# The second attention of a four-block network: where the softmax division is done, and who fixes the order of the vector engines

## The chip, the core and the metric

The kernel runs on one core of one Trainium2 chip. The core has five engines that take their instructions from queues of their own: TensorE (PE in the profile; PEld is its weight load), VectorE (DVE), ScalarE (ACT), GpSimd (POOL) and SyncE (SP, which issues transfers). The metric is the device time of one execution in microseconds; a comparison uses the median of several executions.

## The reference

Six residual blocks follow each other on 8 sequences of 512 rows with 256 columns, all in fp32. The change touches the fifth block, the second kind of attention, and what runs beside it. Each row is normalised first, and the block adds its result to the normalised rows:

```
def _L1_attn_ref(x, w_q, w_k, w_v, w_o):        # 16 heads of 64
    q = jnp.einsum('bsd,hdk->bhsk', x, w_q)
    k = jnp.einsum('bsd,hdk->bhsk', x, w_k)
    v = jnp.einsum('bsd,hdk->bhsk', x, w_v)
    scores = jnp.einsum('bhqk,bhmk->bhqm', q, k) * scale
    weights = jax.nn.softmax(scores, axis=-1)
    z = jnp.einsum('bhqm,bhmk->bhqk', weights, v)
    ...
    return x + z            # z after its heads are joined and multiplied by w_o
...
    x = x + 0.5 * _L1_ffn_ref(_layernorm(x), ...)       # the block before: 16 experts, 4 per row
    x = x + _L1_attn_ref(_layernorm(x), ...)
    x = x + 0.5 * _L1_ffn_ref(_layernorm(x), ...)       # the block after
```

There is no mask. The blocks before and after route every row to 4 of 16 experts; the rows are scattered to slots in memory, multiplied tile by tile, and gathered again.

## The kernel before

The rows stay on the chip in `x` as 32 tiles of 128 rows. `_attn1` (L925) works through 64 chunks; chunk n = 8b + c holds heads 2c and 2c+1 of sequence b. A chunk has two halves of two query tiles each, and the half numbered g = 2n + half is the unit of the loop (L1119 to L1155).

What one chunk needs:

- `heads` (L984): two projections `pq` (L992), the queries copied out by ACT (L998), the keys by DVE (L1000). They are made two chunks ahead.
- `scores` (L1005): per query tile the score matmuls of both heads (L1018) into a pair of banks `sp`, the negated row maxima on DVE (L1024), and two exponentials on ACT (L1027), which also sum each row.
- `turn` (L1032): the exponentials of a query tile are transposed on TensorE (L1039), four blocks per bank for each head, and copied into `eT`. `evict` (L186 to L189) gives head 0 to DVE and head 1 to ACT.
- `products` (L1042): `run` multiplies `eT` with the values (L1052) and lets GpSimd widen the reciprocals of the sums (L1059). `scale` transposes these on TensorE (L1065), copies them with ACT (L1069) and multiplies the product by them on DVE (L1071).
- `value` (L967) and `project` (L1076): the value projections of the coming sequence (L973, copied at L977), and the output projections of the previous one (L1082, added to `x` at L1086).
- `prepare` (L938): the means and variances of some tiles (`ln_range`), normalised rows (L952), `x` plus these rows on GpSimd (L958), and their transposes (L961).

Scores run a half ahead: `scores(g + 1)` is issued before the turns of half g. The products of chunk n are issued in the first half of chunk n + 1, between its scores and its first turn. Projections wait in a list `fill`; one is taken between the two turns of a half, and in each half a share of the rest after the second turn. Two pairs of banks hold scores, one bank the product `zp`, and all turns and projections rotate through three banks with the tag "m".

Other work runs beside it. During the first chunks, results of the block before are added to `x` on DVE (`add`, L1443), four per chunk, each followed by an indirect gather on GpSimd (L1424). In chunk 42 the means, and in chunks 43 to 47 the normalised rows, transposes and logits of the first 20 tiles of the next block are made (`Front.units`, L1817); from chunk 48 on the steps of its `routing` (L1260) run on DVE, five per chunk; in the last 20 halves GpSimd scatters rows (`send`, L1245).

The order on TensorE and GpSimd is the order in which the program issues (`manual_schedule`, L1113). DVE's and ACT's instructions are ordered by the compiler's planner; the adds of L1443 carry one order by hand, behind the last row maximum (`latest`, `behind`).

## Time and profile before

| | |
|---|---|
| median of 3 executions | 4506.57 us (4497.96 to 4514.63) |
| the profiled execution | 4405.38 us, its span 4403.7 us |
| granted clock of TensorE, mean over the span | 0.916 |
| the second attention, first transpose to last output projection | 2655.8 to 3952.8 us |
| PE, PEld, DVE, ACT, POOL busy over the whole span | 88%, 52%, 45%, 33%, 28% |

The profiled execution is about 100 us shorter than the median of the others; the profile doesn't show those. All rows of the profile are of this one execution. In the page, a group gives the line, the engine, the operation, the output and input tiles and their shapes, the count, the busy time with the mean duration in ns, and the idle time of the engine just before, with what ended it. A wait is named by the instruction that waited and the one that ended it. A line of the trace in order of time gives the start, the duration, engine, line and operation, and in brackets the idle time before it. Matmuls overlap, so their durations are latencies: the spacing of weight loads shows their rate.

### The profile page before, as it was taken

To read this page: it belongs to the slowest core of one execution; us is meant where nothing else is said; L and a number is where in the kernel's file an instruction comes from. 1 tells how busy PE (TensorE), PEld (TensorE's weight loads), DVE (VectorE), ACT (ScalarE), POOL (GpSimd) and SP (SyncE) were. 2 spreads that over 40 slices of the span, in tenths; PEclk is the share of its full clock that TensorE was granted. 3 is DMA by queue.
4 is the path that set the end of the run, shared out by engine and by line. 5 is a ranking of instruction groups with operands and counts; after the bars stand their busy time and mean duration, and the time that the engine had idled before them with its cause. 6 is when DMAs were issued, how large, how long until landed. Compare 5 with 4: busy or idle time off the path is not lost.

```text
span 4403.7 us, 51503 instructions
## 1 busy us (share of the span) xinstructions
PE 3892.5 (88%) x17660; PEld 2305.1 (52%) x17660; DVE 1966.9 (45%) x5201; ACT 1437.6 (33%) x3226; POOL 1225.5 (28%) x1132
## 2 busy tenths in 40 slices
PE   5799987999999769999678988999999999998988
PEld 5566653333334546656445664545545555556664
DVE  5221116545554441210464455665555547455355
ACT  2122222433433212222122233544454443442331
POOL 2323323323320223233253141220000020542156
PEclk9999997889996579999689999999999999998999
DMA  5223226500000313232433450100000000133464
GB/s 181 54 59 67 69 38 227 174 22 11 25 20 6 97 34 64 63 66 39 132 121 120 163 177 25 29 27 8 1 1 1 1 1 1 48 115 123 149 187 134
DMA packets 262992, 316.64 MB, mean 72 GB/s; under 512 B 31696, under 2 KB 232784, under 8 KB 262480
## 3 DMA queue, kind: packets, MB, share of 16 engines
q1 hardware_dynamic: 213584, 212.12, 15.4%
q0 software_dynamic: 49152, 101.24, 9.5%
q8 instruction: 145, 2.38, 0.2%
q14 instruction: 111, 0.91, 0.1%
HBM read 157.81 MB, written 147.06 MB: 69 GB/s over the span
## 4 chain that ended last, share of the span: by engine, by line
PE 35%; DVE 7%; issue 4%; DMA 3%; ACT 3%; POOL 1%; SPq 0%; POOLq 0%; DVEq 0%; ACTq 0%
PE pq L992 5%; PE hs L1651 5%; PE sp L1018 5%; PE zp L1052 5%; PE tp L1039 4%; PE pv L973 3%; PE yp L1082 2%; DMA yg<-ys_d,slot 2%; ACT ex L1027 2%; DVE nmax L1024 1%; PE hp L1571 1%; POOL yg L1424 1%; PE yps L1671 1%; DMA acc_d<-ob,idx 1%; DVE xT L189 1%
## 5 line engine op out<-in xcount | busy, mean ns | idle before, releaser
L1027 ACT ACTIVATE ex<-sp,nmax 128x512 f32<-128x512 f32 x512 | 347.3, 689 | 411.5 <-DVE nmax L1024 389.8
L458 PE MATMUL op<-w,hid 128*128 128x256 f32 x2048 | 473.3, 394 | 0.0
L447 PE MATMUL hp<-exT,w 128*128 128x512 f32 x1024 | 447.5, 595 | 0.0
L458 PEld LDWEIGHTS op<-w,hid 128*128 128x128 f32 x2048 | 406.2, 199 | 66.6 <-issue 8.6
L1424 POOL DMA_INDIRECT yg<-ys_d,slot x256 | 262.9, 1027 | 514.5 <-DVE x L1443 222.9
L465 POOL DMA_INDIRECT acc_d<-ob,idx x128 | 199.7, 1560 | 688.6 <-ACT ob L464 383.8
L1651 PE MATMUL hs<-w_sb,xT 128*128 (+1 forms) x1152 | 338.5, 418 | 54.6 <-DVE xT L189 46.0
L463 DVE TENSOR_TENSOR ob<-op,b 128x256 f32<-128x256 f32 x128 | 54.4, 425 | 663.3 <-PE op L458 656.6
L1024 DVE TENSOR_REDUCE nmax<-sp 128x2 f32<-128x1024 f32 x256 | 303.2, 1218 | 72.8 <-PE sp L1018 72.7
L1039 PEld LDWEIGHTS tp<-ident,ex 128*128 128x128 f32 x2048 | 227.6, 142 | 190.8 <-issue 129.6
L447 PEld LDWEIGHTS hp<-exT,w 128*128 128x128 f32 x1024 | 194.7, 192 | 232.0 <-issue 231.2
L1039 PE MATMUL tp<-ident,ex 128*128 128x128 f32 x2048 | 276.2, 278 | 36.3 <-ACT eT L187 35.9
L735 DVE CUSTOM_DVE_ANT_0 junk<-sp,mask 128x128 f32<-128x128 f32 (+3 forms) x512 | 248.7, 486 | 130.1 <-PE sp L728 110.5
L1651 PEld LDWEIGHTS hs<-w_sb,xT 128*128 128x128 f32 x1152 | 205.7, 198 | 175.7 <-DVE xT L189 96.4
L451 ACT ACTIVATE hid<-hp,b 128x512 f32<-128x512 f32 x256 | 175.9, 687 | 337.9 <-PE hp L447 337.9
L1018 PE MATMUL sp<-qk,qk 64*128 64x512 f32 x1024 | 261.4, 630 | 2.2 <-ACT ex L1027 2.2
L1245 POOL DMA_INDIRECT slots_d<-wide,slot x176 | 174.1, 989 | 309.7 <-DMA slots_d<-wide,slot 113.1
L992 PE MATMUL pq<-xnT,wide 128*128 128x512 f32 x512 | 251.2, 614 | 5.8 <-DVE eT L189 5.0
L773 ACT ACTIVATE ex<-st 128x1024 f32<-128x1024 f32 (+3 forms) x256 | 173.9, 703 | 245.6 <-DVE st L771 245.5
L1052 PE MATMUL zp<-eT,v 128*64 128x512 f32 x1024 | 234.9, 600 | 0.3 <-DVE eT L189 0.3
L464 ACT ACTIVATE ob<-ob,gate 128x256 f32<-128x256 f32 x128 | 65.0, 508 | 510.8 <-DVE ob L463 510.8
L1059 POOL COPY wide<-rec 128x512 f32<-128x512 f32 x64 | 39.3, 614 | 672.5 <-PE rp L1065 577.2
(328 smaller groups left out, 6105.9 us busy)
## 6 DMA issues: line engine op xcount, KB each, us to landing
xs<-slots_d SPq DMA_DIRECT2D x70, 512.0 KB, 5.1
ys_d<-ys SPq DMA_DIRECT2D x70, 512.0 KB, 3.5
w<-in_W SPq DMA_DIRECT2D x32, 1024.0 KB, 5.6
slots_d<-mask SPq DMA_DIRECT2D x8, 2304.0 KB, 14.7
ys_d<-mask SPq DMA_DIRECT2D x8, 2304.0 KB, 13.0
w_sb<-in_w SPq DMA_DIRECT2D x24, 512.0 KB, 7.8
xn_d<-xn SPq DMA_DIRECT2D x16, 512.0 KB, 4.3
acc_d<-x SPq DMA_DIRECT2D x8, 1024.0 KB, 5.7
```

Source lines behind the costliest of these rows:

```text
L447: nc.tensor.matmul(hp, lhsT=w1[:, c, f * P : f * P + P], rhs=exT[e][:, c, h * CH : h * CH + CH], start=(c == 0), stop=(c == DC - 1),)
L458: nc.tensor.matmul(op, lhsT=hid[h][:, f, i * P : i * P + P], rhs=w2[:, f, :], start=(f == 0), stop=(f == FC - 1),)
L465: nc.gpsimd.indirect_dma_start(out=acc_d[:, :], out_offset=bass.IndirectOffsetOnAxis(ap=idx[:, e, st : st + 1], axis=0), in_=ob, in_offset ...
L735: nc.vector.tensor_tensor_reduce(out=junk[:, :wd], in0=sps[h // 2][:, h % 2, :wd], in1=mask[:, S - wd :], scale=1.0, scalar=NEG, op0=ALU.a ...
L992: nc.tensor.matmul(pp, lhsT=(wq, wk)[a][:, k, c * P : c * P + P], rhs=seq[b]["xnT"][:, k, :], start=(k == 0), stop=(k == DC - 1),)
L1018: nc.tensor.matmul(sp[:, j, :], lhsT=q[r, qt * P : qt * P + P], rhs=k[r, :], start=True, stop=True)
L1024: latest[0] = nc.vector.tensor_reduce(nmax, sp, AX.X, ALU.max, negate=True).ins
L1027: nc.scalar.activation(ex[:, j, :], sp[:, j, :], AF.Exp, bias=nmax[:, j : j + 1], accum_out=ch["sums"][:, qt, j : j + 1],)
L1039: nc.tensor.transpose(tp[:, k, :], ch["ex", qt][:, j, k * P : k * P + P], self.ident)
L1052: nc.tensor.matmul(zp[DK1 * j : DK1 * j + DK1, :], lhsT=seq[b]["v", h][:, k, at : at + DK1], rhs=ch["eT"][:, j, k, :], start=(k == 0), sto ...
L1424: inst = nc.gpsimd.indirect_dma_start(out=self.y[t][:, r, :], out_offset=None, in_=self.k.ys_d[:, :], in_offset=bass.IndirectOffsetOnAxis( ...
L1651: nc.tensor.matmul(hp.rearrange("p a i -> p (a i)"), lhsT=st[j]["xT"][:, c, :], rhs=self.w13[:, st[j]["e"], c, :].rearrange("p e i -> p (e ...
```

## The change

The exponentials are divided by their row sums before they are turned. `divide(i)` takes the reciprocal of a query tile's two sums and multiplies both heads' rows in place on DVE. The reciprocals' widening, transposes, copy and the product on DVE go; the product `zp` is copied out by ACT (`out`). `evict` gives the turns of even query tiles to DVE and of odd ones to ACT.

The order of DVE and ACT is now that of the program too. In a half: scores and maxima of the next half with the exponentials of its first tile, the products or the adds, the even turn, the exponentials of its second tile, the copy of the product, one step beside, one projection, the first division, the odd turn, a step, the other projections, the second division, a step. The adds move from the first half to the second and start in chunk 0.

Means of `x` that were taken in one go (`ln_range` at sequences 3 and 5, and `Front.stats`) are taken two tiles at the end of a chunk (`own`). A sequence's normalisation, transposes, value projections and the output projections are spread over its chunks by a fixed table: normalisation at c = 0, transposes at c = 1, values 2, 1, 1, 2, 1, 1 at c = 2 to 7, output projections two at c = 1 and two at c = 2. Routing runs six steps per chunk.

```diff
@@ -938,24 +938,22 @@
         def prepare(b):
             st = seq[b] = {"z": []}
-            def norm(c):
+            def normal():
+                mv, rstd = stats
+                st["xn"] = work.tile([P, QT, D], F32, name="xn", bufs=1)
+                st["xnT"] = work.tile([P, DC, CH], F32, name="xnT")
 ...
+                rows = self.x[:, b * QT : b * QT + QT, :]
+                nc.gpsimd.tensor_tensor(rows, rows, st["xn"], ALU.add)
+            def turned(c):
                 def run():
-                    mv, rstd = stats
-                    if c == 0:
-                        if b in (0, 3, 5):
-                            self.ln_range(pool, stats, b * QT, {0: 3, 3: 2, 5: 3}[b] * QT)
-                        st["xn"] = work.tile([P, QT, D], F32, name="xn", bufs=1)
-                        st["xnT"] = work.tile([P, DC, CH], F32, name="xnT")
 ...
-                        nc.gpsimd.tensor_tensor(rows, rows, st["xn"], ALU.add)
                     tp = psum.tile([P, CH], F32, name="tpn", tag="m", bufs=3)
                     for i in range(QT):
                         nc.tensor.transpose(
@@ -977,9 +975,10 @@
                     nc.vector.tensor_copy(st["v", h][:, i, :], pp)
                 return run
-            return [norm(c) for c in range(DC)] + [
-                value(i, h) for h in range(HK // CH) for i in range(QT)
-            ]
+            v = [value(i, h) for h in range(HK // CH) for i in range(QT)]
+            return [[normal], [turned(0), turned(1)], v[0:2], v[2:3], v[3:4], v[4:6], v[6:7], v[7:8]]
         def heads(n):
             b, c = divmod(n, NC)
@@ -1004,11 +1003,10 @@
         def scores(g):
             n, half = divmod(g, 2)
             ch, q, k = chunk[n], chunk[n][0], chunk[n][1]
-            if half == 0:
-                ch["sums"] = work.tile([P, QT, 2], F32, name="sums", bufs=3)
-            sps = []
+            sps, nmax, sums = [], [], []
             for i in range(2):
                 qt = 2 * half + i
                 sp = psum.tile([P, 2, CH], F32, name="sp", tag="s", bufs=2)
@@ -1019,15 +1017,28 @@
                         sp[:, j, :], lhsT=q[r, qt * P : qt * P + P], rhs=k[r, :], start=True, stop=True
                     )
             for i, sp in enumerate(sps):
-                qt = 2 * half + i
-                nmax = work.tile([P, 2], F32, name="nmax", bufs=4)
-                latest[0] = nc.vector.tensor_reduce(nmax, sp, AX.X, ALU.max, negate=True).ins
-                ex = ch["ex", qt] = work.tile([P, 2, CH], F32, name="ex", bufs=4)
+                m = work.tile([P, 2], F32, name="nmax", bufs=4)
+                nc.vector.tensor_reduce(m, sp, AX.X, ALU.max, negate=True)
+                nmax.append(m)
+                sums.append(work.tile([P, 2], F32, name="sums", bufs=4))
+                ch["ex", 2 * half + i] = work.tile([P, 2, CH], F32, name="ex", bufs=4)
+            def exps(i):
                 for j in range(2):
                     nc.scalar.activation(
-                        ex[:, j, :], sp[:, j, :], AF.Exp,
-                        bias=nmax[:, j : j + 1], accum_out=ch["sums"][:, qt, j : j + 1],
+                        ch["ex", 2 * half + i][:, j, :], sps[i][:, j, :], AF.Exp,
+                        bias=nmax[i][:, j : j + 1], accum_out=sums[i][:, j : j + 1],
                     )
+            def divide(i):
+                rec = work.tile([P, 2], F32, name="rec", bufs=2)
+                nc.vector.reciprocal(rec, sums[i])
+                for j in range(2):
+                    row = ch["ex", 2 * half + i][:, j, :]
+                    nc.vector.tensor_scalar(row, row, rec[:, j : j + 1], None, ALU.mult)
+            exps(0)
+            return exps, divide
         def turn(n, qt):
             ch = chunk[n]
@@ -1037,12 +1048,13 @@
                 tp = psum.tile([P, QT, P], F32, name="tp", tag="m", bufs=3)
                 for k in range(QT):
                     nc.tensor.transpose(tp[:, k, :], ch["ex", qt][:, j, k * P : k * P + P], self.ident)
-                self.evict(ch["eT"][:, j, :, qt * P : qt * P + P], tp, j)
+                self.evict(ch["eT"][:, j, :, qt * P : qt * P + P], tp, qt)
         def products(n):
             b, c = divmod(n, NC)
             ch = chunk[n]
+            box = []
             def run():
                 zp = psum.tile([P, CH], F32, name="zp", tag="z", bufs=1)
@@ -1053,25 +1065,14 @@
                             zp[DK1 * j : DK1 * j + DK1, :], lhsT=seq[b]["v", h][:, k, at : at + DK1],
                             rhs=ch["eT"][:, j, k, :], start=(k == 0), stop=(k == QT - 1),
                         )
-                rec = work.tile([P, QT, 2], F32, name="rec", bufs=3)
-                nc.vector.reciprocal(rec, ch["sums"])
-                wide = work.tile([P, QT, 2, DK1], F32, name="wide", bufs=1)
-                nc.gpsimd.tensor_copy(wide, bc(rec, 3, DK1))
-                ch["wide"], ch["zp"] = wide, zp
-            def scale():
-                rp = psum.tile([P, CH], F32, name="rp", tag="m", bufs=3)
-                for qt in range(QT):
-                    nc.tensor.transpose(
-                        rp[:, qt * P : qt * P + P], ch["wide"][:, qt].rearrange("p h d -> p (h d)"), self.ident
-                    )
-                rs = work.tile([P, CH], F32, name="rs", bufs=1)
-                nc.scalar.copy(rs, rp)
+                box.append(zp)
+            def out():
                 zn = work.tile([P, CH], F32, name="zn", bufs=9)
-                nc.vector.tensor_tensor(zn, ch["zp"], rs, ALU.mult)
+                nc.scalar.copy(zn, box[0])
                 seq[b]["z"].append(zn)
-            return [run, scale]
+            return [run, out]
         def project(b):
             def out(i):
@@ -1089,70 +1090,95 @@
             return [out(i) for i in range(QT)]
         front = Front(self, after, ctx)
-        latest = [None]
         def row_psum(cols):
             t = psum.tile([P, CH], F32, name="row", tag="m", bufs=3)
             return t[:, :cols]
-        steps = after.routing(0, front.lg, front.pool, row_psum, lambda: None)
+        known = []
+        steps = after.routing(0, front.lg, front.pool, row_psum, lambda: known.append(True))
         groups = after.parts[0] // QT
-        def ahead(n):
-            i = n - (NC * groups + 2)
-            if i == 0:
-                front.stats()
-            elif 1 <= i <= groups:
-                return front.units(i - 1, row_psum)
-            elif groups < i:
-                advance(steps, 5)
-            return []
-        with tc.manual_schedule(engines={mybir.EngineType.PE, mybir.EngineType.Pool}):
-            for piece in prepare(0) + heads(0) + heads(1):
+        def moments(pool, stats, t):
+            return lambda: self.ln_moments(pool, stats, t, 2)
+        own = {}
+        for first, tiles, n in ((3 * QT, 2 * QT, 10), (5 * QT, 3 * QT, 25)):
+            for t in range(0, tiles, 2):
+                own[n] = moments(pool, stats, first + t)
+                n += 1
+            own[n] = lambda first=first, tiles=tiles: self.ln_finish(pool, stats, first, tiles)
+        begin = NC * groups + 2
+        for t in range(0, after.parts[0], 2):
+            own[33 + t // 2] = moments(front.pool, after.stats, t)
+        assert len(own) == 4 + 6 + 2 + after.parts[0] // 2 and max(own) == begin
+        last = own[begin]
+        own[begin] = lambda: (last(), self.ln_finish(front.pool, after.stats, 0, after.parts[0]))
+        E = mybir.EngineType
+        with tc.manual_schedule(engines={E.PE, E.DVE, E.Activation, E.Pool}):
+            self.ln_range(pool, stats, 0, 3 * QT)
+            for piece in sum(prepare(0), []) + heads(0) + heads(1):
                 piece()
-            scores(0)
-            fill, tail, behind = [], [], None
+            exps, divide = scores(0)
+            exps(1)
+            divide(0)
+            divide(1)
+            fill, tail = [], []
             coming = prepare(1)
             for n in range(N):
                 b, c = divmod(n, NC)
                 if c == 0:
-                    coming = prepare(b + 1) if b + 1 < B else []
+                    coming = prepare(b + 1) if b + 1 < B else [[]] * NC
                 if n + 2 < N:
                     fill += heads(n + 2)
-                if c not in (3, 4):
-                    fill += coming[:2]
-                    coming = coming[2:]
-                fill += ahead(n)
+                fill += coming[c]
+                if 1 <= n - begin <= groups:
+                    fill += front.units(n - begin - 1, row_psum)
+                def ahead():
+                    if n > begin + groups:
+                        advance(steps, 1)
                 for half in range(2):
                     g = 2 * n + half
                     if g + 1 < 2 * N:
-                        scores(g + 1)
+                        exps, divide = scores(g + 1)
                     if half == 0 and tail:
                         tail.pop(0)()
-                    if half == 0 and n > 0:
+                    if half == 1:
                         for _ in range(min(TOPK, len(beside))):
-                            beside.pop(0)(behind)
-                    t = 2 * n + half - 2 * N + after.parts[0]
+                            beside.pop(0)()
+                    t = g - 2 * N + after.parts[0]
                     if t >= 0:
+                        assert known
                         front.send(t)
-                    behind = latest[0]
                     turn(n, 2 * half)
+                    more = g + 1 < 2 * N
+                    if more:
+                        exps(1)
                     if half == 0 and tail:
                         tail.pop(0)()
+                    ahead()
                     if fill:
                         fill.pop(0)()
+                    if more:
+                        divide(0)
                     turn(n, 2 * half + 1)
-                    left = 2 - half
-                    for _ in range(-(-len(fill) // left)):
+                    ahead()
+                    for _ in range(len(fill) if half else max(0, len(fill) - 3) // 2):
                         fill.pop(0)()
+                    if more:
+                        divide(1)
+                    ahead()
+                if n in own:
+                    own[n]()
                 tail = products(n)
-                if c == 0 and b > 0:
-                    fill += project(b - 1)
+                if b > 0 and c < 2:
+                    fill += project(b - 1)[2 * c : 2 * c + 2]
             for piece in tail + project(B - 1):
                 piece()
@@ -1803,9 +1829,6 @@
         self.lg = self.pool.tile([P, f.parts[0], E1], F32, name="chosen")
         self.xn = {}
-    def stats(self):
-        self.k.ln_range(self.pool, self.f.stats, 0, self.f.parts[0])
     def normal(self, t, n):
         if t % QT == 0:
```

## The prediction

> **What bounds the kernel now.** I read the granted clock first (0.916 over the run, 0.96 to 1.00 in this stage), then busy time by engine over one sequence of the second attention, then TensorE's waits, then a single chunk in order of time. A batch is one sequence: 8 chunks of 2 heads, c = 0 to 7.
>
> Busy time from one sequence's first projection to the next (length; busy us of PE, PEld, DVE, ACT, POOL; clock):
>
> ```profile
> 3164.41:3320.42 156.01, 152.16 (x714) 80.84 (x713) 82.48 (x113) 70.95 (x178) 7.22 (x9) 1.00 0.00 1
> ```
>
> TensorE is nearly full, DVE and ACT half empty. The waits from 2680 to 3930 (us, times, longest):
>
> ```profile
> PEld tp L1039 <- ACT eT L187: 57.6, 63, 2.1
> PEld sp L1018 <- ACT ex L1027: 15.6, 31, 2.8
> PEld zp L1052 <- DVE x L1443: 9.9, 13, 0.8
> ```
>
> The largest wait is turning (L1039) behind ACT's copies. A light chunk (c=3 or 4) in order of time shows where:
>
> ```profile
> 3231.70 0.47 PEld L1065 LDWEIGHTS rp<-ident,wide 128*128 128x128 f32 x4
> ...
> 3238.82 1.29 PEld L1039 LDWEIGHTS tp<-ident,ex 128*128 128x128 f32 x12 [0.76 <-issue]
> 3241.32 0.42 PEld L1039 LDWEIGHTS tp<-ident,ex 128*128 128x128 f32 x4 [1.20 <-ACT eT L187]
> ```
>
> In its second half no projection stands between the two turns. They need four banks of three, and ACT's copy lies behind exponentials: 1.20 us lost. Starts of the head products, one per chunk:
>
> ```profile
> 3227.30 3.65 PE L1052 MATMUL zp<-eT,v 128*64 128x512 f32 x16
> 3243.82 3.65 PE L1052 MATMUL zp<-eT,v 128*64 128x512 f32 x16
> 3262.60 3.65 PE L1052 MATMUL zp<-eT,v 128*64 128x512 f32 x16
> ```
>
> A light chunk takes 16.52 us, one with two value projections 18.78. Their four matmul records each, at a cadence of 0.43, are 3.42 together; 18.78 - 3.42 = 15.36, so the light chunk loses about 1.2, as the wait says.
>
> Durations by shape:
>
> ```profile
> L1024 DVE TENSOR_REDUCE nmax<-sp 128x2 f32<-128x1024 f32 x256 | 303.2, 1218 | 72.8 <-PE sp L1018 72.7
> L189 DVE COPY eT<-tp 128x512 f32<-128x512 f32 x253 | 171.2, 685 | 84.1 <-PE tp L1039 84.0
> L1443 DVE SCALAR_TENSOR_TENSOR x<-yg,coef,x 128x256 f32<-128x256 f32 x72 | 34.5, 480 | 1.1
> L334 DVE TENSOR_SCALAR vals<-high,at x2: 353/354/354, 84.3 to 1548.3; 128x256 f32<-128x256 f32 x2
> ```
>
> [...] L334 (one pointer scalar) takes 354 ns, the 128x256 copy from PSUM 424. [...] weight loads around scores start 0.95 us apart against 0.43; this order is kept, so these losses stay. [...]
>
> **The change part by part.**
>
> *Removed.* Per chunk four transposes rp (about 0.5 us of TensorE: 0.47 of loading, 0.43 of streaming), ACT's copy rs (0.59), POOL's widening (0.61), DVE's product zn (0.69). zn becomes an ACT copy (estimate 0.6, from rs), which releases zp with no chain through POOL and TensorE. Only the 0.5 is on the path: 4.0 per batch.
>
> *Added on DVE.* Per half chunk two divisions D: reciprocal 128x2 plus two multiplies 128x512. Reciprocals of 8 and 16 columns take 203 and 253 ns, so two columns about 165. Multiply: L334's 354 plus 256 elements [...] (the copies within SBUF show 226 ns at 128 columns and 326 at 320, 0.52 ns each) = 487 ns; [...] upper end 690, the PSUM copy. I take 487: [...] D = 1.1 to 1.2 us. DVE per light chunk, with back-to-back spacing (max 1.18, copies 0.64): 4x1.18 + 4x0.64 + 4x1.1 + key copy 0.66 = 12.3, against TensorE's 16.52 - 1.2 - 0.5 = 14.8.
>
> *Fixed order: half 0.* Times from the first score load, offsets as in the trace: maxima 1.17 to 3.53; products 1.92 to 5.50; even turn at 5.50; its two DVE copies 6.20 to 7.48; D, D to 9.7 (10.0 at D = 1.2). TensorE reaches the next scores at 9.16, and their first maximum is wanted at 10.33: DVE is ready 0.3 to 0.6 early. The products shelter DVE here.
>
> *Half 1.* Maxima to 3.53; copies 4.17 and 4.81; the odd turn wants its bank at 4.13 with a projection now ahead of it: no stall worth counting. Key copy 5.47, D 6.6, value copy 8.1, D 9.2, against scores at 7.4: the next maximum is 0.7 late, but half 0 wants its copies only at 6.2, so nothing is lost. The turns' new wait, for rows divided half a chunk before, never comes last.
>
> *Gain.* Per batch four chunks (c = 0, 3, 4, 7) lose 1.2 and the rest about 0.5 together = 5.3; with rp 9.3. New: at c=1 and 2 the key projection waits for the query copy, which ACT holds behind the second exponentials (0.7 each), small gaps 0.3: 1.7. Net 7.6 per batch, 0.95 per chunk.
>
> *Moved: the adds.* Each of 18 chunks has four (L1443), with four gathers behind them on POOL. They now stand in half 1 between maxima and copies, in fixed order. Spacing 0.40: 1.6 us. The odd turn's bank comes at 5.85, not 4.17: 1.35 lost, 0.15 at the second bank, about 0.2 at the value's. 18 x 1.6 = 29. Before, they cost nothing: sequences with adds took 156.6 us, without 156.0. Their gathers wait behind the same adds, two chunks ahead of use; POOL loses its widenings; no DMA moves on SP's queue.
>
> *Moved: routing.* Six steps per chunk in fixed places. Summing the rows of L1269 to L1415 gives about 37 us of DVE, of which chunk 48 gets 5.4, chunk 51 9.1, chunk 52 9.9 (one step, the picks L1366/L1369, alone 4.8). With 12.3 plus value copy or normalisation these reach 19.2, 22.1, 22.9 against 14.8, 16.5, 16.5: DVE bounds them, 4.5 + 5.6 + 6.4 = 16.5. Before, that sequence lost 8.5 (products 3654.89 to 3816.40 = 161.5 against 156): net 8.
>
> *Moved: means, projections, normalisation.* Two tiles of means are 1.2 us at chunk ends, inside half 0's shelter (1.9 us are left); the three finishes make DVE wait for ACT's square root and its 1.28 us table: 1.5 to 2 late once; with the longer serial start I charge 4. If the shelter is gone, the 10 chunks of means before the front cost 12. Output projections two per chunk cost the same on TensorE. DVE waits behind a projection's result before D at c=1, 2: 0.25 late, counted among gaps. Sends on POOL (6.6 us a tile) fit in a half of 7.4.
>
> *Sum against the profiled run.* 64 x 0.95 = 61 gained. Light tail chunks 57 to 62 gain 1.7 rather than 0.95: 4. The first 18 chunks ran 3 over the later rate: taken as gained. 68 - 29 - 8 - 4 = 27 us. The span is 4403.7 (execution 4405.4); the median of timed runs is 4506.6, 101 longer, with no trace of where. I subtract the same 27: 4479.6, a clock difference aside.
>
> **Rivals.**
> - *DVE is full: break even.* More gaps of a few tenths per chunk, or adds and routing that cost half as much again (+19): 4490 to 4525. For it: 12.3 of 14.8 in fixed order. Against: both halves fit with slack.
> - *Slower: the multiply is slow and maxima come late.* Half 0's slack is 0.3 to 0.6. At 690 ns with D = 1.65, the chain ends at 10.8, 0.5 late in every chunk: 64 x 0.5 = 32, routing +3 chunks x 2.2 = 7: 4519; beyond about 720 ns it is over 0.5% slower. For it: reductions in front, [...]. Against: L334.
> - *Adds and routing are absorbed.* With no loss there, 27 + 29 + 8 = 64 gained: 4443. Against: three banks and strict order leave no way round the adds.
> - *No change in what binds.* If projections removed the 1.2 us stall but turns still met late copies, only rp's 32 less 41: about 4516.
>
> **How the numbers follow.** A difference under 0.5%, 22 us, can't be told from none. Forecast's mechanism 0.54 (its own range 4455 to 4492), absorbed 0.07, break even 0.21, slow multiply 0.12, stall stays 0.06. Part of the forecast's range lies within 22 us. So faster 0.54, same 0.30, slower 0.16. Range 4442 to 4521: from absorption to the 690 ns multiply.
>
> **What would show it.** Multiplies near 490 ns; chunks with one value projection near 16.6 us, with none near 14.9; no wait of turns on ACT copies over 0.5; chunks with adds about 1.6 longer than later ones, with a turn waiting on DVE's copy; chunks 48, 51, 52 over 19. Wrong if maxima start over 1.5 us after their scores in half 1 everywhere, if multiplies take over 620, or if the clock falls below 0.95 here.

## The result, and the profile after

The changed kernel takes 4485.33 us (median of 20 runs, 4459.21 to 4496.58); the kernel before, run beside it, 4508.8 us (4479.09 to 4527.67, 20 runs). The ratio is 0.9944 with a 95% interval of 0.9927 to 0.996: some 25 us faster, between 18 and 33. Forecast were 27 us; the time lies in the range forecast, and a gain of over 0.5% was its likeliest case.

The two profiled executions stand the other way round: 4403.7 us of span before, 4479.3 after. Most likely they come from two chips: in the later runs the kernel before has a median of 4406.09 us on chip number 6 and of 4498.0 on number 5. The difference lies outside the stage in question: the first head product of the attention starts at 2701.63 us before and at 2749.65 after (48 us later), and from the last output projection to the end 450.9 us pass before and 496.0 after (45 more). All comparisons of the attention below therefore go by the stamps of the head products, one per chunk, from the first to the last. A second profile of the kernel before shows how well they repeat: 1232.8 us against 1232.7.

| part of the attention (head products counted from 1) | before | after | difference | forecast |
|---|---|---|---|---|
| 1 to 19, chunks with adds | 353.1 | 364.2 | +11.0 | +9 to +12 |
| 19 to 41, ordinary chunks | 416.6 | 394.8 | -21.7 | -21 |
| 41 to 57, the next block's front and the routing | 345.1 | 342.1 | -3.0 | -7 |
| 57 to 64, the last chunks | 117.9 | 114.2 | -3.8 | -10.6 |
| whole | 1232.7 | 1215.2 | -17.5 | |

The forecast column is the prediction's sum cut at the same places: 0.95 us a chunk, +29 for the adds (with or without the 3 us that the first chunks ran over), +8 for the routing, -4 for the tail. Its 4 us for means, finishes and the longer start belong to no row.

The differences are taken before rounding. The timed gain (18 to 33) and the gain by stamps (17.5) just miss each other. About 1 us lies ahead of the first stamp: from the last matmul of the block before to the first head product 53.7 and 53.1 us pass in the two profiles of the kernel before, 52.4 in that of the changed one. The rest, a few us, was not traced.

Busy time over one ordinary sequence of the changed kernel, from head product to head product (length; busy us and instructions of PE, PEld, DVE, ACT, POOL; clock, DMA share, GB/s):

```profile
3212.89:3360.77 147.88, 147.24 (x683) 76.88 (x681) 110.84 (x216) 72.40 (x180) 2.37 (x1) 1.00 0.00 1
```

A sequence took 156.0 us before, with DVE busy for 82.5; now it takes 147.88 with DVE at 110.84. TensorE has 31 matmul records less (the transposes of the reciprocals are 32) and hardly idles.

The waits of the attention (us, times, longest):

```profile
PEld tp L1050 <- DVE eT L189: 69.9, 90, 3.5
DVE x L1087 <- PE yp L1083: 57.9, 25, 2.9
ACT zn L1072 <- PE yp L1083: 43.3, 7, 12.2
```

The turns' largest wait was for ACT's copy (57.6 us); now it is for DVE's. The third line has no counterpart before, and its longest entry comes up again below.

A light chunk in order of time, weight loads first (its second half), then DVE (from the first half's maxima to the second's):

```profile
3270.79 0.86 PEld L1050 LDWEIGHTS tp<-ident,ex 128*128 128x128 f32 x8 [0.76 <-issue]
...
3273.05 0.14 PEld L1050 LDWEIGHTS tp<-ident,ex 128*128 128x128 f32 x1 [0.28 <-DVE eT L189]
3273.44 0.79 PEld L1050 LDWEIGHTS tp<-ident,ex 128*128 128x128 f32 x7 [0.25 <-issue]
```

```profile
3262.54 2.32 DVE L1021 TENSOR_REDUCE nmax<-sp 128x2 f32<-128x1024 f32 x2
3266.02 1.29 DVE L189 COPY eT<-tp 128x512 f32<-128x512 f32 x2 [1.16 <-PE tp L1050]
3267.22 0.16 DVE L1035 RECIPROCAL rec<-sums 128x2 f32<-128x2 f32 x1
3267.42 0.88 DVE L1038 TENSOR_SCALAR ex<-ex,rec 128x512 f32<-128x512 f32 x2
3268.21 0.15 DVE L1035 RECIPROCAL rec<-sums 128x2 f32<-128x2 f32 x1
3268.40 0.88 DVE L1038 TENSOR_SCALAR ex<-ex,rec 128x512 f32<-128x512 f32 x2
3270.05 2.35 DVE L1021 TENSOR_REDUCE nmax<-sp 128x2 f32<-128x1024 f32 x2 [0.76 <-PE sp L1016]
```

The 1.20 us before the odd turn's last four loads are gone. One division takes 0.99 us from reciprocal to reciprocal (3267.22 to 3268.21), and DVE still waits 0.76 us for the scores of the second half: the slack that the prediction put at 0.3 to 0.6.

The head products around it, and the multiplies of the divisions by shape:

```profile
3261.67 3.65 PE L1064 MATMUL zp<-eT,v 128*64 128x512 f32 x16
3278.22 3.65 PE L1064 MATMUL zp<-eT,v 128*64 128x512 f32 x16
3294.76 3.65 PE L1064 MATMUL zp<-eT,v 128*64 128x512 f32 x16
```

```profile
L1038 DVE TENSOR_SCALAR ex<-ex,rec 128x512 f32<-128x512 f32 x512 | 242.8, 516 | 8.9
```

Chunks c = 3 and 4 take 16.55 and 16.54 us as before, but each now holds a value projection. An ordinary chunk without one takes 14.65.

### The profile page after: what moved, and what is told of

Same layout as the page of the kernel before. It is cut to its first block, busy times and chain, and to the rows that moved or that the text cites. A ratio compares the mean times of both kernels' runs of the same rounds, so it can differ in the third digit from the quotient of the medians.

```text
span 4479.3 us, 51528 instructions
## 1 busy us (share of the span) xinstructions
PE 3885.8 (87%) x17404; PEld 2281.6 (51%) x17404; DVE 2159.3 (48%) x5841; ACT 1429.7 (32%) x3226; POOL 1193.9 (27%) x1068
## 3 DMA queue, kind: packets, MB, share of 16 engines
q1 hardware_dynamic: 213584, 212.12, 15.2%
## 4 chain that ended last, share of the span: by engine, by line
PE 35%; DVE 9%; issue 4%; DMA 2%; ACT 2%; another core or an unknown queue 1%; POOL 1%; SPq 0%; POOLq 0%; DVEq 0%; ACTq 0%
PE hs L1677 6%; PE zp L1064 5%; PE sp L1016 4%; PE tp L1050 4%; PE pq L991 4%; PE pv L971 3%; PE yp L1083 2%; PE yps L1697 2%; PE hp L1597 2%; DVE nmax L1021 2%; DMA yg<-ys_d,slot 1%; ACT ex L1028 1%; DVE x L1469 1%; PE yp L1619 1%
## 5 line engine op out<-in xcount | busy, mean ns | idle before, releaser
L1677 PE MATMUL hs<-w_sb,xT 128*128 (+1 forms) x1152 | 346.9, 426 | 93.2 <-DVE xT L189 53.5
L1038 DVE TENSOR_SCALAR ex<-ex,rec 128x512 f32<-128x512 f32 x512 | 242.8, 516 | 8.9
L1685 DVE TENSOR_TENSOR as<-sgs,hs 128x128 f32<-128x128 f32 x288 | 82.3, 286 | 307.5 <-ACT sgs L1683 269.1
```

The costliest lines, as they stand in the source:

```text
L1038: nc.vector.tensor_scalar(row, row, rec[:, j : j + 1], None, ALU.mult)
L1677: nc.tensor.matmul(hp.rearrange("p a i -> p (a i)"), lhsT=st[j]["xT"][:, c, :], rhs=self.w13[:, st[j]["e"], c, :].rearrange("p e i -> p (e ...
```

## The experiments

Where an experiment was made by an edit of the changed kernel, its lines are those of that kernel.

### The kernel before once more

> The kernel before, unchanged. The profile of before ran 4405 us while the other executions had a median of 4509. If the 100 us lie outside the second attention, a second profile shows the attention's 1233 us from the first head product to the last again, within 5 us, and the difference in the expert blocks in front of it and behind it. If the attention itself varies, the 1233 us change by 20 or more and the comparison of the two attentions in the two profiles says little.

It took 4384.97 us in its one execution, and its attention 1232.8 us, part by part within 0.2 us of the first profile. So differences of 1 us between stamps mean something in most parts. Around the routing they do not: the part from 41 to 57 takes 342.1 us in the changed kernel and 340.4 in the one with ten buffers (below), whose edit doesn't touch it. Both profiles of the kernel before show the shorter time; that the attention doesn't depend on the chip is seen from the changed kernel and its variants, whose ordinary chunks agree to 0.02 us on chips with the shorter and with the longer time.

### The adds in the first half

```diff
-                    if half == 1:
+                    if half == 0:
                         for _ in range(min(TOPK, len(beside))):
                             beside.pop(0)()
```

> The kernel after with one edit: the four adds per chunk stand in the first half of a chunk, behind the maxima and the products, instead of in the second. Theory (three banks and a fixed order make the adds delay the odd turn in the second half, while in the first half DVE idles 1.2 to 2.0 us for the products): chunks 1 to 17 fall from 18.5 us to about 16.6 with one value projection, those with two from 21.9 to 18.3; 33 to 38 us less than after in all, a ratio to before near 0.986. Rival (DVE is simply full, where the adds stand doesn't matter): less than 10 us gained over after, ratio 0.993 to 0.996.

4352.52 us against 4406.09 for the kernel before, ratio 0.9882 (0.986 to 0.9905). The first part fell from 364.2 to 333.3 us, the other parts by 1.6 at most; the attention took 1182.0, 33.2 less than in the changed kernel, where 33 to 38 were expected. A chunk with adds, in the changed kernel first:

```profile
2814.37 2.36 DVE L1021 TENSOR_REDUCE nmax<-sp 128x2 f32<-128x1024 f32 x2 [0.76 <-PE sp L1016]
2816.64 2.04 DVE L1469 SCALAR_TENSOR_TENSOR x<-yg,coef,x 128x256 f32<-128x256 f32 x4
2818.59 1.28 DVE L189 COPY eT<-tp 128x512 f32<-128x512 f32 x2
2819.33 0.42 PEld L1050 LDWEIGHTS tp<-ident,ex 128*128 128x128 f32 x4 [2.24 <-DVE eT L189]
```

and in this one:

```profile
2755.29 2.35 DVE L1021 TENSOR_REDUCE nmax<-sp 128x2 f32<-128x1024 f32 x2
2757.56 2.04 DVE L1469 SCALAR_TENSOR_TENSOR x<-yg,coef,x 128x256 f32<-128x256 f32 x4
2759.86 1.29 DVE L189 COPY eT<-tp 128x512 f32<-128x512 f32 x2 [0.26 <-PE tp L1050]
```

The same 2.04 us stand between maxima and copies in both. In the first half TensorE is busy with the head products meanwhile, and DVE even waits 0.26 us for the turn. In the second half nothing covers them, and the odd turn waits 2.24 us for its bank. The theory held: the adds cost 31 us by their place alone.

### A dearer multiply

```diff
-                    row = ch["ex", 2 * half + i][:, j, :]
-                    nc.vector.tensor_scalar(row, row, rec[:, j : j + 1], None, ALU.mult)
+                    for s in range(0, CH, CH // 2):
+                        row = ch["ex", 2 * half + i][:, j, s : s + CH // 2]
+                        nc.vector.tensor_scalar(row, row, rec[:, j : j + 1], None, ALU.mult)
```

> The kernel after with each multiply of a 512-wide row made in two pieces of 256, so that the same work takes about 700 ns instead of 480 to 516: some 0.45 us more per division, 1.8 us of DVE per chunk, 115 us in all. Theory (DVE has about 0.8 us of slack before the maxima of the second half and 1.2 before the even turn's copies of the first): chunks without adds or routing grow by 0.1 to 0.3 us, chunks 48, 51 and 52 by 1.5 to 2 each, in all 12 to 30 us slower than after. Rival (DVE bounds the stage): 80 to 115 us slower than after.

4403.61 us, ratio to before 0.9999 (0.9988 to 1.001); the attention 1229.9 us, 14.7 over the changed kernel. By the timed ratios it is about 25 us over, by the stamps 15; both lie in the theory's 12 to 30. The rival's 80 and more is no fair measure, since it took 0.45 us more per division: the edit added 0.26 (below), 67 us of DVE in all. Of these 67, 15 to 25 reached the time, so DVE doesn't bound the stage as a whole. A light chunk here:

```profile
3227.38 1.15 DVE L1039 TENSOR_SCALAR ex<-ex,rec 128x256 f32<-128x256 f32 x4
3228.43 0.16 DVE L1035 RECIPROCAL rec<-sums 128x2 f32<-128x2 f32 x1
3228.63 1.14 DVE L1039 TENSOR_SCALAR ex<-ex,rec 128x256 f32<-128x256 f32 x4
3230.01 2.36 DVE L1021 TENSOR_REDUCE nmax<-sp 128x2 f32<-128x1024 f32 x2 [0.24 <-PE sp L1016]
```

Each division is 0.26 us longer, and the slack shrinks from 0.76 to 0.24 as it should: twice 0.26. The chunk stays at 16.55. Dearer are chunks in which DVE was already behind: with adds up to 20.15 instead of 18.50, and in the routing (346.9 instead of 342.1).

### The division alone, in the old order

Reciprocal and multiplies are put behind the exponentials of the kernel before; the widening, the transposes, `rs` and DVE's product go, and ACT copies the product.

```diff
+                rec = work.tile([P, 2], F32, name="rec", bufs=2)
+                nc.vector.reciprocal(rec, ch["sums"][:, qt, :])
+                for j in range(2):
+                    nc.vector.tensor_scalar(ex[:, j, :], ex[:, j, :], rec[:, j : j + 1], None, ALU.mult)
...
-                nc.vector.tensor_tensor(zn, ch["zp"], rs, ALU.mult)
+                nc.scalar.copy(zn, ch["zp"])
```

> The kernel before with the division alone: rows divided on DVE before the turns, the product copied by ACT, no widening, no transposes of reciprocals; the planner still orders DVE and ACT, and adds, means, projections and routing stand where they stood. Theory (two separate gains of like size: 0.5 us per chunk of removed transposes, 0.65 us per chunk of stalls that only the fixed order with a projection between the turns removes): 32 us gained by the transposes, the 1.2 us stall in light chunks still there or longer, since the turns now wait for divisions as well; 10 to 30 us faster than before in all. Rival (the division is the whole of it): 40 us or more faster than before. Rival (the order is the whole of it, and the division costs as much as it saves): no faster than before.

4373.29 us, ratio 0.9932 (0.9911 to 0.9953): as much as the whole change. The attention took 1211.5 us. A sequence takes 151.71 us, a light chunk 15.92 instead of 16.53. So the old scaling with its transposes cost 0.61 us in seven chunks of eight; the chunk with the output projections gained nothing (32.69 us before, 32.68 here). The stall is where it was:

```profile
3190.93 1.29 PEld L1043 LDWEIGHTS tp<-ident,ex 128*128 128x128 f32 x12 [0.76 <-issue]
3193.42 0.42 PEld L1043 LDWEIGHTS tp<-ident,ex 128*128 128x128 f32 x4 [1.20 <-ACT eT L187]
```

The chunks with adds take 345.1 us here, 19 less than in the whole change. In the chunk whose head products run from 2701.36 to 2705.01, the planner starts the adds at 2701.34 (two), 2703.39 and 2705.07, so beside the head products or next to them.

### The fixed order alone, with the old scaling

The divisions are taken out of the changed kernel, the widening, transposes, `rs` and product put back; the output projections stand at c = 1 again.

```diff
-                nc.scalar.copy(zn, box[0])
+                rp = psum.tile([P, CH], F32, name="rp", tag="m", bufs=3)
...
+                nc.scalar.copy(rs, rp)
+                nc.vector.tensor_tensor(zn, box[0], rs, ALU.mult)
...
-                if b > 0 and c < 2:
-                    fill += project(b - 1)[2 * c : 2 * c + 2]
+                if b > 0 and c == 0:
+                    fill += project(b - 1)
```

> The fixed order, the early means and the spread value projections with the old scaling: no divisions on DVE, but again four transposes, a copy on ACT and a product on DVE per chunk; the four output projections of a sequence all stand in c = 1, as in the kernel before. My theory: the transposes cost 64 x 0.5 = 32 us of TensorE, and DVE, which loses some 4.4 us of divisions per chunk and takes back 0.7, gives back 12 of the 22 us lost around the routing. Chunks with adds stay 1.3 to 2 us longer than later ones, since the adds stand between the maxima and the turn's copies with or without divisions. Attention from first to last head products 1225 to 1245 us against 1215 with the whole change and 1233 before; time within 0.6% of the kernel before. Rival: it is the divisions that make the adds dear. Then the first 18 chunks fall from 364 us to 345 or so in spite of the transposes, and the attention ends under 1215.

4513.39 us against 4498.0, ratio 1.0026 (1.0009 to 1.0043). The attention took 1230.6 us, with the first part at 370.8: a light chunk with adds 19.17 us against 17.21 without, the same 1.96 as in the whole change (18.50 against 16.54). The rival fell: the divisions do not make the adds dear. Of the 12 us that were to come back around the routing, 6.7 did: chunks 48 to 54 take 15.2 us more than ordinary ones of the same kernel, where the whole change takes 21.9 more. Most of it came in chunk 51 (2.2 over instead of 5.6). Chunk 52 kept 9.5 of its 10.1, though DVE is busy there for 17.98 us instead of 21.09.

One number was unforeseen: from the last head product to the last output projection 29.5 us pass, 18.0 to 18.5 in every other kernel. Here the widening of the reciprocals stands on GpSimd behind the scatters, in the program's order:

```profile
3994.19 0.98 POOL L1279 DMA_INDIRECT slots_d<-xn,slot  x1 [0.65 <-DMA slots_d<-xn,slot]
3995.17 0.62 POOL L1068 COPY wide<-rec 128x512 f32<-128x512 f32 x1
3995.84 0.72 PEld L1074 LDWEIGHTS rp<-ident,wide 128*128 128x128 f32 x4 [10.30 <-POOL wide L1068]
```

Together, per ordinary sequence: 156.01 us before, 151.71 with the division alone, 152.05 with the order alone, 147.88 with both. 4.30 and 3.96 are gained apart, 8.13 together: here the two parts add up.

### What removed the stall: the projection between the turns, or who copies

Two edits. The first takes the projection of each second half (the key's; in c = 1 and 2 the query's) from between the turns (with ten `zn` buffers, as in the next section); the second gives each turn's copies to DVE and ACT by head, as before.

```diff
-                    if fill:
+                    if fill and half == 0:
                         fill.pop(0)()
```

> The changed kernel with ten zn buffers and, in every second half, the key projection moved from between the two turns to behind them: the old neighbourhood of the turns with the new order of the copies. My theory: the 1.20 us stall of the light chunks went because a projection now stands between the turns. Without it the odd turn's second bank waits for DVE's copy of the even turn, which lies behind the maxima: about 0.7 to 0.9 us late by the stamps of a light chunk, so that chunks c = 0, 3, 4, 5, 6, 7 grow by 0.6 to 0.9 us (16.54 to 17.2 or 17.4), and the attention by 35 to 55 us against 1208. Rival: the stall went because the even turn's copies no longer stand behind ACT's exponentials. Then the chunks stay within 0.2 us of 16.54.

```diff
-                self.evict(ch["eT"][:, j, :, qt * P : qt * P + P], tp, qt)
+                self.evict(ch["eT"][:, j, :, qt * P : qt * P + P], tp, j)
```

> The changed kernel with the copies of the turned rows shared as before, one head of each turn on DVE and one on ACT, where the change gives the even turn to DVE and the odd turn to ACT. My theory: with the projection between the turns the copies have time on either engine, and ACT's second pair of exponentials can wait: light chunks stay within 0.3 us of 16.54, the attention within 15 us of 1215. Rival: it is the sharing that keeps the copies on time; then the light chunks lose the 1.2 us again and the attention is over 1250.

Each was executed once: 4472.47 and 4383.44 us, beside 4397.19 for the kernel before. Without the projection between them light chunks take 17.53 us, 0.99 more, and the attention 1287.9, 79.5 over the same kernel with it. The direction was right, the size short (35 to 55): each ordinary chunk lost 0.7 to 1.2 us, and those with adds 1.7 on average (the light ones take 18.89 or 20.59 for 18.50). In the part with adds the key projection behind the turns took 1.89 us in one of the chunks of 18.89 (at 2834.53) and 3.43 in one of those of 20.59 (at 2853.42), so that the loss there need not be the wait alone. The second half of a light chunk:

```profile
3275.15 1.29 PEld L1050 LDWEIGHTS tp<-ident,ex 128*128 128x128 f32 x12 [0.76 <-issue]
3277.42 0.42 PEld L1050 LDWEIGHTS tp<-ident,ex 128*128 128x128 f32 x4 [0.97 <-DVE eT L189]
```

The old picture with another releaser. With the copies by head, light chunks stay at 16.54 and 16.55, the attention takes 1213.3 us. So the stall went because work for TensorE stands between the turns; who copies is indifferent there. It is not indifferent where DVE is late: chunks with adds take 17.86 us with the copies by head (18.50 by turn), those with two values 19.57 (21.92), while the part with the routing is 10 us longer (352.5 for 342.1).

### Ten buffers for the head pairs' products

```diff
-                zn = work.tile([P, CH], F32, name="zn", bufs=9)
+                zn = work.tile([P, CH], F32, name="zn", bufs=10)
```

> The changed kernel with ten buffers for the products of a head pair (zn) in place of nine. My theory: the 12 us wait of ACT in chunk 58 is for the last output projection of the sequence before, which in the last sequence, without value projections, has slipped to the chunk's second half; with a tenth buffer the chunk falls from 26.8 us to 21.3 to 22 and nothing else moves: attention 1210 us against 1215. Rival: the copy waits for something else (the single bank of head products). Then chunk 58 stays over 26.

Chunk 58 fell from 26.76 to 21.56 us, the part 57 to 64 from 114.2 to 109.0, the attention to 1208.4; its one execution took 4464.25 us. What chunk 58 of the changed kernel shows:

```profile
3886.06 0.42 PEld L1050 LDWEIGHTS tp<-ident,ex 128*128 128x128 f32 x4 [2.52 <-DVE eT L189]
3887.50 4.97 PEld L1083 LDWEIGHTS yp<-wide,zn 128*128 128x128 f32 x16 [1.02 <-DVE eT L189]
3888.76 0.59 ACT L1072 COPY zn<-zp 128x512 f32<-128x512 f32 x1 [12.17 <-PE yp L1083]
```

ACT's copy of the product of chunk 57 needs the buffer of the first product of sequence 6, and the last output projection of that sequence reads it. While the sequence has value projections, that projection lies in the chunk's first half; in the last sequence it slips to the second. ACT's other copies wait behind the product's, and the turns for them.

### The routing spread over other chunks

Steps per place, six places a chunk; the picks, one step of 4.8 us, become two.

```diff
-                    if n > begin + groups:
-                        advance(steps, 1)
+                    advance(steps, share.pop(0))
...
+            48: (1, 0, 0, 1, 1, 0), 49: (4, 4, 0, 1, 1, 0), 50: (4, 4, 0, 1, 0, 0),
+            51: (1, 0, 0, 1, 0, 0), 52: (1, 0, 0, 1, 0, 0), 53: (1, 0, 0, 0, 1, 0),
```

> The changed kernel with the routing's steps placed by chunk: 3 in chunk 48, 10 in 49 and 9 in 50 (most of them in the first half, where the output projections keep TensorE busy for 3.4 us each), 2 each in 51 and 52, the picks cut in two steps in 53. My theory: the routing is DVE work that overflows the light chunks 51 and 52 (5.6 and 10.1 us over) while 49 and 50 have 7 and 10 us free on DVE. The excess over an ordinary sequence falls from 21.9 us to 6 to 12; chunks 51 and 52 go below 18.5. Rival: the steps hurt by their place in the order wherever they stand. Then 49 and 50 grow by what 51 and 52 lose, and the excess stays within 4 us of 21.9.

4476.7 us in one execution; attention 1211.3. Chunks 48 to 54 take over ordinary ones, in turn: 3.1, 1.2, 0.9, 5.6, 10.1, 1.1, 0 in the changed kernel and 2.2, 3.2, 3.0, 3.2, 0.3, 1.3, 2.5 here: 22 against 15.7, so the theory's 6 to 12 was missed, and chunk 51 stayed at 19.73 where under 18.5 was expected. Chunk 58 takes 28.38 instead of 26.76, for a reason that no run shows; so the attention gained only 3.9. Two windows show both sides, chunk 52 of the changed kernel and chunk 52 of this one (columns as above):

```profile
3756.97:3783.58 26.61, 18.54 (x81) 8.64 (x79) 21.09 (x48) 8.68 (x22) 9.06 (x9) 0.87 0.10 35
```

```profile
3764.98:3781.86 16.88, 16.64 (x79) 7.99 (x77) 13.91 (x27) 8.59 (x22) 0.00 (x0) 1.00 0.00 0
```

In the first, TensorE, which needs 16.5 us, waits for DVE; 8.07 us of it are a single wait, shown in the part on why. In the second, without the picks and what follows them, the chunk is TensorE's again. But the places taken, though in chunks where TensorE is busy with output projections, cost 4 us of the 12 saved in 51 and 52, and one step that fell to chunk 54, with a matmul between DVE operations, another 2.5. Place counts, not only the sum.

### All of it together

Adds in the first half, ten buffers, the routing spread (with four of the steps of chunks 49 and 50 in the second half), and the projections of c = 1 and 2 in the order output, query, output, key.

```diff
-                    fill += heads(n + 2)
+                    q, k = heads(n + 2)
+                    fill += late[:1] + [q] + late[1:] + [k]
...
-                if b > 0 and c < 2:
-                    fill += project(b - 1)[2 * c : 2 * c + 2]
+                late = project(b - 1)[2 * c : 2 * c + 2] if b > 0 and c < 2 else []
```

> Adds in the first half, ten zn buffers, routing spread, and in chunks c = 1 and 2 the query and key projections put between the output projections (output, query | output, key in place of output, output | query, key), so that the key projection no longer finds its bank held by ACT's copy of the query. My theory: 33 us from the adds, 5 from the buffer, 10 to 15 from the routing and about 1 us in each of 14 chunks from the order: attention 1150 to 1162 us against 1215; c = 1 at 22.0 to 22.5 us against 23.1 and c = 2 at 24.7 to 25.2 against 25.7. Time 4325 to 4345 us where the kernel before takes 4406. Rival: the gains overlap, since what is taken from TensorE's waits shows up as DVE's limit: attention over 1170.

4430.48 us against 4498.0 on this chip (number 5), ratio 0.9848 (0.9827 to 0.9869), the fastest of the kernels against its own base. The attention took 1165.5 us, 50 under the changed kernel and 3.5 over the upper end expected: c = 1 and 2 gave 0.67 each (22.44 and 25.00), but in the last sequence the same order costs 2.4 (chunks 57 and 58 together 45.5 instead of 43.1 with ten buffers alone), and the routing's chunk 49, with four of its steps in the second half, takes 27.05, 0.7 more than with the first placing in spite of the better order. The absolute times expected (4325 to 4345) were for chip 6; 67.5 us under before here, against 61 to 81 there.

## Why the prediction was right, and where not

**The time.** 4480 forecast, 4485.33 measured: its mechanism was right in the main, and the timed gain of 25 is near the 27 of its sum. That it is so near is in part luck. Against the stamps' 17.5 the sum is 9.5 too high: 7 in the last chunks, 4 around the routing and 2 in the first part, less the 4 charged for means and start, which nothing shows; and of the timed 25, some 6 lie where nothing was traced.

**Removed transposes.** 0.5 us a chunk forecast, 4.0 a sequence; 4.30 measured with the division alone: 0.61 us in seven chunks of eight, nothing in the one with the output projections.

**The stall of 1.20 us.** Forecast gone, because a projection stands ahead of the odd turn. Shown on both sides: it stays with the division alone (1.20), goes with the order, and comes back as 0.97 when the projection is taken away. The rival in which the stall stays (4516) fell with that. The step's net, 5.3 less 1.7, is 3.6 a sequence; the order alone gave 3.96. "Net 7.6 per batch" became 8.13.

**The multiply.** 487 ns were forecast, L334's 354 and 0.52 ns for each of 256 more columns, with 690 as the upper end. The median of its 512 records is 486: the 256 columns more than L334's cost 132 ns, where copies out of PSUM take 261 for as many (685 at 512 columns, 424 at 256). Some far longer records (below) lift the mean to 516. The division was a little cheaper than forecast, 0.99 us for 1.1 to 1.2, since the second multiply starts 0.40 us after the first, before that one has ended. So the rival "slow multiply" (4519) fell. The division by halves (1.25 us) shows what a dearer one would have cost: the ordinary chunks still had slack for it, the others took the whole gain, which is the "break even" of the rival "DVE is full", reached by another way.

**The adds.** 29 us forecast, 31 measured, and the waits named there (a turn on DVE's copy) were seen. At the first bank the turn waits 2.24 us, 1.96 more than in an ordinary chunk, where 1.35 was reckoned; by the prediction's own times (5.85 against 4.13) it would have been 1.7. Their spacing was taken as 0.40, 1.6 us for the four; it is 0.52, 2.04 for the four, and the kernel before already showed it in most pairs, two in 1.00 us. The sentence "three banks and strict order leave no way round the adds" was true of that place only: half a chunk earlier they cost next to nothing.

**The routing.** Here the sum failed, and in one chunk the mechanism too. Forecast were 16.5 us over, 8.5 of which the kernel before was said to lose too. The 8.5 does not follow from the numbers beside it: 161.5 less 156 is 5.5. Counted by chunks 48 to 54, the kernel before lost 9.3 and the changed one 21.9, so the net was 12.6 and not 8. Chunk 48 was 3.0 over (4.5 reckoned) and stayed at 17.7 us, not over 19; chunk 51 was 5.6 over, as reckoned, and chunk 52 10.1 where 6.4 were reckoned (3.9 and 10.9 in two variants with the same routing); 49, 50 and 53 were 3.2 over together, where nothing was. In chunk 52 the picks stand in front of the maxima, and TensorE's own order holds a matmul of the routing (L1417), which waits for what DVE does after both:

```profile
3766.35 1.48 DVE L1392 TENSOR_TENSOR pick<-hots,left 128x640 f32<-128x640 f32 x1
3771.22 2.35 DVE L1021 TENSOR_REDUCE nmax<-sp 128x2 f32<-128x1024 f32 x2
3775.24 0.58 PE L1417 MATMUL row<-ident,number 128*1 128x128 f32 x2 [8.07 <-DVE number L1415]
```

From 3772 to 3778 the granted clock is 0.50, and the key projection behind that matmul takes 3.21 us, where the query projections at 3761.48 and 3788.09 take 1.88. With the order alone DVE has some 3 us less to do in chunks 51 and 52; chunk 51 lost 2.2, but chunk 52 still 9.5. So the sum of DVE's work, by which the prediction reckoned, fits chunk 51; in chunk 52 the order of the steps decides. How much the place of that matmul costs by itself was not tested.

**The last chunks.** 10.6 us forecast, 3.8 measured. The step that failed is "zn becomes an ACT copy ..., which releases zp with no chain". It took out one chain and overlooked another: the copy's own buffer, one of nine, is released by an output projection which the change had moved a chunk further. The two moves were priced apart, at nothing each; together they cost 5.2 us, of 6.8 that are missing. With the ACT copy and the old place of the projections (the division alone) chunk 58 takes 15.9 us and shows no such loss.

**Means, normalisation and start.** 4 us were charged. The stamps show nothing: chunks 25 to 28, which hold means, take 23.11, 25.67, 16.55 and 16.55 us like any others, and the time up to the first head product did not grow either (above). That the means lie in the shelter of the first half, as was named, fits this.

**c = 1 and 2.** 0.7 us each for a key projection that waits for the query's copy: 0.67 each came back when the order was changed.

**The other cases.** "Adds and routing absorbed" (4443) was against the profile of the changed kernel, but within reach by a better place: moving the adds alone brings the ratio to 0.9882. What the change as a whole hides is that its two parts differ: by the timed ratios the division brings 0.9932 by itself, the fixed order 1.0026; the order's gain in ordinary chunks is given back by the adds, the routing and the last sequence.

## What to carry to other kernels

When an order is fixed by hand, ask of each piece of side work what the pacing engine does meanwhile: four operations of 2 us together cost 31 us over the kernel in one half of a chunk and next to nothing in the other. A move that delays the last reader of a rotating buffer has to be priced together with every new writer of that buffer, above all at the end of the loop, where the work that kept the reader early runs out. Where the pacing engine itself waits in its own order for a result of the side work, the sum of the side work is no measure of what it costs (chunk 52). And where two parts of a change hit different waits (here TensorE's own instructions and a bank wait), measure each alone: they may add up in the steady state, while only one of them pays outside it.

## What was not expected of the hardware

- *DVE's multiply takes longer beside GpSimd's add.* The residual add of GpSimd (128x1024) comes once per sequence, and in five of the eight it meets the divisions:

```profile
3213.26 2.37 POOL L953 TENSOR_TENSOR x<-x,xn 128x1024 f32<-128x1024 f32 x1 [146.82 <-DVE rec L1035]
3213.29 3.01 DVE L1038 TENSOR_SCALAR ex<-ex,rec 128x512 f32<-128x512 f32 x2
```

  Two multiplies that take 0.88 us elsewhere take 3.01; the longer one is 2.62 us, and ends 0.28 us after GpSimd's add. It is the same at 3064.11, 3361.17, 3509.04 and 3685.22. Where the same add meets maxima, which read PSUM (2751.66 and 2901.82), these keep their 1.21 us. The delay at 3213.29 falls under the head products, and the turn behind them starts after the same 0.81 us as in the light chunk (3216.47, 3265.25). Near the end of the routing it shows from the other side too: a normalisation of GpSimd (L1261) that starts beside two multiplies at 3791.50 takes 2.06 us where the median of these is 1.22, and the two multiplies 1.37.
- *Adds into the same rows follow each other at 0.51 to 0.52 us, multiplies on different rows at 0.40 with the same 0.48 of duration.* That the dependence on the row is the reason was not tested.
- *Chips differ by 100 us with one kernel*: 4406.09 us on chip 6, 4397.19 on chip 1 (one execution), 4498.0 on chip 5. The profiles put the difference ahead of the second attention and behind it. The mean granted clock of an execution doesn't sort them: 0.906 in the one on chip 1, and 0.906 in one of 4509.83 us on chip 5. What makes the difference stays open.
